# Moving shared experts, row sends and joins around the last sorting of a decoder layer

## The chip, the cores and the metric

The kernel runs on one core of a Trainium2 chip, as one program. The metric is the device time of one execution in microseconds, lower is better. The core has TensorE (PE), VectorE (DVE), ScalarE (ACT) and GpSimd (POOL), and SyncE (SP), which issues DMAs only. Each engine works through its own queue in order; the engines wait for each other by semaphores.

## The reference

One layer of a pre-norm decoder over 8 batches of 512 tokens of width 256, in float32. Three residual steps follow one another, each on the layer-normed x:

```
x = x + attn(layernorm(x))       # 16 heads: softmax over the tokens, causal convolution with it, output projection
x = x + xattn(layernorm(x), ctx) # causal cross attention over ctx_1024
x = x + ffn(layernorm(x))        # mixture of experts
```

The feed-forward part is where the change lies:

```
out    = sum over 2 shared experts of (silu(x wg_s) * (x wu_s)) wd_s          # width 128 each, for all tokens
probs  = softmax(x router_w)                                                  # 16 routed experts
weights, indices = top_k(probs, 2); weights = weights / (sum(weights) + 1e-9)
out   += sum over a token's 2 experts of weight * (silu(x wg_e) * (x wu_e)) wd_e   # width 64 each
```

## The kernel before, in words

**Batches.** A loop over the 8 batches runs the attention parts. The order inside an iteration is a written list of names (`ORDER`): steps of batch b (no sign), of the next one (`+`), and leftovers of the batch before (`-`). The leftovers are its shared experts (`-h0 -h1 -d0 -d1`), its ranking (`-rk`) and its sends (`-sd0` to `-sd7`).

**Shared experts** (`steps_shared`). Two steps `hidden` (gate and up matmuls, L614, a tanh, two scalings on VectorE, L618 and L619) and two steps `down` (L631), added into the batch's x tile. For batches 0 to 5 the x tile is then written out to DRAM (`kept`, L636).

**Routing.** A batch's tokens are ranked by expert (`ranked`, L554 to L580), and eight indirect DMAs on GpSimd (`send`, L588) put their normed rows into the DRAM buffer `xg` of their group, sorted by expert. Batches 0 to 5 are group 0, batches 6 and 7 group 1. When a group's last batch is ranked and sent, `tiled` and `tabled` (L645 to L706) work out a table of tiles of 128 rows, each of one expert: where its rows begin and which expert it has. This stretch, from the ranking to the first tile of a group, is called its sorting.

**Routed experts** (`steps_routed`). Tiles go four at a time (a quad): `fetch` loads the rows (`xs`, L718, on SP), `pick` copies the expert's gate and up weights (ScalarE, L727) and loads its down weights (`wdn`, L737, on SP and ScalarE), `turn` transposes the rows (L753), `hidden` and `down` are the matmuls (L772, L786), a scaling by the routing weight follows (L797, L799), and `put` (L807) writes the rows by indirect DMAs on GpSimd to `yg`, four for a quad, in the order of the tokens. Group 0 has 16 quads, group 1 has 8. The scaled rows of group 0 pass through 8 buffers (`y`).

**Joins** (`steps_join`). For a batch, `keep` loads the kept x again (L842), `take` loads its two rows for each token from `yg` (L851), `join` adds both on VectorE (L860) and writes the output (L861).

**Order around the change.** Where one list of steps is to be spread over another, `merged` interleaves them evenly and `idle(n)` puts in n empty places. The first six quads of group 0 run inside iteration 6, the next eight inside iteration 7 (the list `quads` counts pipeline steps: step q has the turn of q+1, the hidden of q, the down of q-1 and puts of q-1 and q-2). Behind the loop stands batch 7's sorting, with the rest of group 0, the shared experts of batches 6 and 7, and the first joins around it; then group 1's quads with the other joins; then group 1's own takes and joins. `tc.issue_after(x)` holds the steps under it behind instruction x. The written order sets priorities and dependences; a scheduler in the language orders each engine's queue from it when the program is built.

```
sorting = [last["rk"], *idle(3), *send, first1[0], *idle(0), *first1[1:-1], *idle(2), first1[-1]]
for f in merged(sorting, gap + sh, [*idle(0), *old[:5]]):
    f()
```

Here `first1` holds group 1's `tiled`, `tabled`, its first four fetches, `pick(0)` and `turn(0)`; `gap` is the rest of group 0's quads, `sh` the shared experts, `old` the keeps, takes and joins of group 0.

**Buffers that the change touches.** `xT` (4 buffers) holds transposed inputs, `h` (3) the hidden values of the shared experts and some temporaries, `wdn` (3) the down weights of a quad, and in PSUM `gu` (3) serves the hidden and down matmuls of shared and routed experts.

## Time and profile before

| what | us |
|---|---|
| median of 3 runs | 577.05 (573.98 to 578.42) |
| profiled execution | 575.53, of it the span 573.8 |
| PE busy | 508.6 (89% of the span) |
| DVE / POOL / ACT busy | 370.1 / 231.7 / 190.6 |
| mean granted PE clock | 0.949 of full speed |
| DMA | 107.67 MB, mean 188 GB/s |

The profile is one execution. In rows of a timeline the columns are start, length, engine, line, operation, tiles written and read, shape and count; the bracket holds the idle time of the engine just before and what ended it. In a table by stretches each row gives the length, then the busy time of PE, PE's weight loads, DVE, ACT and POOL, the granted PE clock, the share of time in which the DMA engines were busy, and GB/s. The slices of the page cut the span into 40 equal parts of 14.3 us, a digit for each in tenths. Issuing a DMA counts as busy on GpSimd only. Matmuls overlap at their ends, so their lengths add to more than their spacing.

### The profile page before, as it was taken

What the parts mean: (1) busy time and instruction counts of PE and PEld (TensorE: products, weight loads), DVE (VectorE), ACT (ScalarE), POOL (GpSimd) and SP (SyncE); (2) the same over time, 40 slices, a digit from 0 to 9 for tenths busy, and PEclk for the clock granted to TensorE, in tenths of its full rate; (3) what the DMA queues carried; (4) which work ended last, traced back from release to release, by engine and by line L of the source; (5) the groups of instructions that cost most, each with busy time, mean ns of one, the idle gap of its engine ahead of it and who ended that gap; (6) DMA issues with size and microseconds to landing.
All of it is one profiled execution on the core that took longest, in us unless ns stands there. A gap on an engine that the chain in (4) does not pass through costs nothing.

```text
span 573.8 us, 10065 instructions
## 1 busy us (share of the span) xinstructions
PE 508.6 (89%) x3172; PEld 337.0 (59%) x3172; DVE 370.1 (64%) x1290; ACT 190.6 (33%) x483; POOL 231.7 (40%) x257
## 2 busy tenths in 40 slices
PE   8989988999999999999999799999988986898720
PEld 5646626656666675774765367685766643486510
DVE  4348748868769778877876585546854682465343
ACT  2333303322333324224221335445455322156210
POOL 2300503432440640621433412454777577127780
PEclk8999999999999999999999799999999897899665
DMA  8880280751491392194182359756675143768966
GB/s 272 264 320 4 80 297 28 257 227 54 165 335 47 115 324 117 67 312 194 40 298 106 116 155 312 239 162 211 211 239 173 60 154 116 222 185 254 308 247 219
DMA packets 64108, 107.67 MB, mean 188 GB/s; under 512 B 8902, under 2 KB 37580, under 8 KB 63954
## 3 DMA queue, kind: packets, MB, share of 16 engines
q1 hardware_dynamic: 51672, 83.87, 44.4%
q0 software_dynamic: 7680, 16.87, 8.1%
q10 hardware_dynamic: 4704, 6.29, 3.3%
q8 instruction: 25, 0.41, 0.3%
q14 instruction: 27, 0.22, 0.1%
HBM read 82.35 MB, written 34.38 MB: 203 GB/s over the span
## 4 chain that ended last, share of the span: by engine, by line
PE 52%; DMA 17%; DVE 13%; POOL 7%; issue 5%; ACT 2%; SPq 2%; POOLq 0%; ACTq 0%; DVEq 0%
PE pc L398 6%; PE pd L631 4%; PE psc L450 4%; PE pa L479 4%; DMA T<-zd 4%; PE pgu L772 4%; PE pv L366 4%; PE pu L614 3%; PE pt L256 3%; PE pq L354 3%; POOL yg L807 3%; PE pv L338 3%; PE pg L614 3%; DMA xg<-row,place 3%; DMA yg<-y,to 3%
## 5 line engine op out<-in xcount | busy, mean ns | idle before, releaser
L807 POOL DMA_INDIRECT yg<-y,to x96 | 99.2, 1033 | 84.3 <-ACT y L797 50.3
L240 POOL TENSOR_TENSOR rs<-ve,power 128x2 f32<-128x2 f32 x48 | 35.4, 745 | 181.5 <-DVE ve L239 181.3
L588 POOL DMA_INDIRECT xg<-row,place x64 | 64.7, 1011 | 26.4 <-issue 16.2
L398 PE MATMUL pc<-T,vh 128*32 128x256 f32 (+1 forms) x512 | 58.1, 490 | 3.1 <-DMA T<-zd 1.6
L772 PE MATMUL pgu<-xsT,wgu 128*64 128x128 f32 x768 | 54.4, 284 | 2.6 <-DVE rh L776 2.1
L772 PEld LDWEIGHTS pgu<-xsT,wgu 128*64 128x64 f32 x768 | 44.7, 140 | 11.3 <-issue 7.8
L479 PE MATMUL pa<-v,pT 128*128 128x256 f32 x160 | 42.1, 394 | 0.0
L450 PE MATMUL psc<-kT,qT 128*128 128x128 f32 (+3 forms) x128 | 40.6, 441 | 0.7 <-DVE kT L261 0.7
L225 DVE BATCH_NORM_STATS2 bn<-x 128x6 f32<-128x256 f32 x96 | 37.7, 413 | 4.2 <-DMA x<-in_x_dram 3.2
L398 PEld LDWEIGHTS pc<-T,vh 128*32 128x32 f32 x512 | 19.0, 109 | 33.1 <-issue 19.0
L338 PE MATMUL pv<-wv_sb,xr 128*128 128x272 f32 (+1 forms) x128 | 34.1, 413 | 4.2 <-ACT xr L331 4.2
L786 PE MATMUL py<-wdn,rh 64*128 64x256 f32 x192 | 32.5, 428 | 5.7 <-DMA wdn<-wdn_d 4.9
L479 PEld LDWEIGHTS pa<-v,pT 128*128 128x128 f32 x160 | 30.1, 196 | 10.9 <-issue 3.8
L799 DVE TENSOR_SCALAR y<-py,w 128x256 f32<-128x256 f32 x48 | 22.2, 478 | 20.0 <-ACT y L797 12.7
L614 PE MATMUL pu<-x2T,wu_sb 128*128 128x512 f32 x64 | 32.0, 621 | 2.6 <-DVE h L618 2.6
L614 PE MATMUL pg<-x2T,wg_sb 128*128 128x512 f32 x64 | 32.7, 614 | 1.5 <-DVE h L618 1.5
L727 ACT COPY wgu<-wgu_r 128x256 f32 x96 | 32.2, 402 | 5.3 <-ACT rh L774 1.6
L631 PE MATMUL pd<-wd_sb,h 128*128 128x256 f32 x128 | 33.3, 387 | 0.5 <-DVE rh L776 0.5
L753 PE MATMUL pxt<-ident,xs 128*128 128x128 f32 x192 | 29.4, 288 | 4.3 <-DMA xs<-xg 3.8
L244 DVE TENSOR_SCALAR xn<-x,mv,rs 128x256 f32<-128x256 f32 x64 | 28.0, 475 | 6.4 <-POOL rs L240 5.5
L338 PEld LDWEIGHTS pv<-wv_sb,xr 128*128 128x128 f32 x128 | 24.8, 199 | 11.4 <-ACT xr L331 5.4
L432 PE MATMUL po<-wo_sb,oT 128*128 128x256 f32 x128 | 30.2, 389 | 1.0 <-DVE vh L343 1.0
(174 smaller groups left out, 913.5 us busy)
## 6 DMA issues: line engine op xcount, KB each, us to landing
T<-zd SPq DMA_DIRECT2D x32, 1024.0 KB
xs<-xg SPq DMA_DIRECT2D x96, 129.0 KB
x<-in_x_dram SPq DMA_DIRECT2D x8, 512.0 KB
ctxT<-in_ctxT_dram SPq DMA_DIRECT2D x8, 512.0 KB
yj_qT<-yg SPq DMA_DIRECT2D x8, 512.0 KB
yj_v<-yg SPq DMA_DIRECT2D x8, 512.0 KB
xg<-blank SPq DMA_DIRECT2D x6, 516.0 KB
kept<-x ACTq DMA_DIRECT2D x6, 512.0 KB
```

The costliest lines, as they stand in the source:

```text
L225: nc.vector.bn_stats(stats["bn"][:, c, :], src[:, c, :])
L240: st[b].setdefault(("pow", n), []).append(nc.gpsimd.tensor_tensor(stats["rs"][:, lo:hi], ve[:, lo:hi], power[:, lo:hi], ALU.pow).ins)
L338: nc.tensor.matmul(pv[:, :w], xr[:, k, i, :], wv_sb[:, k, :w], start=(k == 0), stop=(k == KC - 1))
L398: nc.tensor.matmul(s["pc"][o][32 * g:32 * g + 32, 2 * jp * P:], vh[:, jp, h, :], s["T"][h // HPT][:, h % HPT, :S - 2 * jp * P], start=(jp ...
L450: nc.tensor.matmul(pc[:, :w], s["qT"][:, k, i * P:w], s["kT"][:, k, :w], start=(k == 0), stop=(k == KC - 1))
L479: nc.tensor.matmul(pa[:, :D], s["pT", i][:, j * P:(j + 1) * P], s["v2"][:, j, :], start=(j == 0), stop=(j == i))
L588: ins = nc.gpsimd.indirect_dma_start(out=grp[g]["xg"][:, :], out_offset=bass.IndirectOffsetOnAxis(ap=s["place"][:, r, c:c + 1], axis=0), i ...
L614: nc.tensor.matmul(p, w[:, k, mt * P:(mt + 1) * P], s["x2T"][:, k, :], start=(k == 0), stop=(k == KC - 1))
L631: nc.tensor.matmul(pd[:, i, :], s["h", mt][:, c * P:(c + 1) * P], wd_sb[:, mt, :], start=(mt == 0), stop=(mt == NSH - 1))
L772: nc.tensor.matmul(p[o * MR:(o + 1) * MR, n, j, :], wgu[:, i, n, k, :], xT[:, k, i, :], start=(k == 0), stop=(k == KC - 1))
L786: nc.tensor.matmul(py[o][:, j, :], h[o * MR:(o + 1) * MR, j, :], wdn[o * MR:(o + 1) * MR, j, :], start=True, stop=True)
L807: ins = nc.gpsimd.indirect_dma_start(out=G["yg"][:, :], out_offset=bass.IndirectOffsetOnAxis(ap=G["to", q][:, i:i + 1], axis=0), in_=G["y" ...
```

## The change

Three lists and some tags change; no arithmetic does.

- The shared experts of batch 5 leave iteration 6 (before, they filled it as leftovers); those of batches 5, 6 and 7 run behind the loop: 5 beside batch 7's ranking and sends, 6 behind them, 7 among group 1's quads.
- Iteration 6 takes seven steps of group 0's quads in place of six, iteration 7 the next eight, so one less is left behind the loop.
- The x tile of batch 5 stays in its buffer (as those of 6 and 7 do), so it is neither kept out nor loaded again.
- Behind the loop the written order has the ranking, then at once the eight sends and group 1's table; `keep` and `take` of the first batches follow group 0's last puts; every join is held behind the last instruction of group 1's table.
- Every second `wdn` of group 1 uses an `h` buffer, and the kept tiles come back into two buffers (`xn1`, `ctxT`) in place of three.

```diff
+LATE = (5, 6, 7,)
+STAY = (5, 6, 7)
...
-                if cp == 1 and b in GROUPS[0]:
+                if cp == 1 and b not in STAY:
...
-        nc.vector.tensor_scalar_mul(G["col"], pt[:1, P:P + T], float(MR))
+        G["col_ins"] = nc.vector.tensor_scalar_mul(G["col"], pt[:1, P:P + T], float(MR)).ins
...
-                wdn = sb.tile([P, QT // 2, D], F32, tag="wdn", bufs=3, name=f"wdn{g}_{q}")
+                wdn = sb.tile([P, QT // 2, D], F32, tag="h" if g and q % 2 else "wdn", bufs=3, name=f"wdn{g}_{q}")
...
-                x = sb.tile([P, NT, D], F32, tag=("xn1", "ctxT", "oT")[bi % 3], bufs=1, name=f"xj{b}")
+                x = sb.tile([P, NT, D], F32, tag=("xn1", "ctxT")[bi % 2], bufs=1, name=f"xj{b}")
...
-                x, y = G["xj", bi] if g == 0 else st[b]["x"], G["yj", bi]
-                for r in range(2):
-                    nc.vector.tensor_tensor(x, x, y[r], ALU.add)
+                x, y = st[b]["x"] if b in STAY else G["xj", bi], G["yj", bi]
+
+                with tc.issue_after(grp[1]["col_ins"]):
+                    for r in range(2):
+                        nc.vector.tensor_tensor(x, x, y[r], ALU.add)
...
-        return [keep(bi) for bi in range(n) if g == 0], [take(bi) for bi in range(n)], [join(bi) for bi in range(n)]
+        return [keep(bi) for bi in range(n) if GROUPS[g][bi] not in STAY], [take(bi) for bi in range(n)], [join(bi) for bi in range(n)]
...
-        late = ("-h0", "-h1", "-d0", "-d1") if b == B - 1 else ()
+        late = ("-h0", "-h1", "-d0", "-d1") if b - 1 in LATE else ()
...
-            now = merged(now, first[:1] + idle(4) + first[1:-1] + idle(22) + first[-1:] + flat(quads[:6]))
+            now = merged(now, first[:1] + idle(4) + first[1:-1] + idle(26) + first[-1:] + flat(quads[:7]))
         elif b == 7:
-            now = merged(now, flat(quads[6:14]))
+            now = merged(now, flat(quads[7:15]))
...
-    gap = flat(quads[14:])
-    sh = [x[n] for x in (sh6, sh7) for n in ("h0", "h1", "d0", "d1")]
-    sorting = [last["rk"], *idle(3), *send, first1[0], *idle(0), *first1[1:-1], *idle(2), first1[-1]]
-    for f in merged(sorting, gap + sh, [*idle(0), *old[:5]]):
+    sh = [shared[b][n] for b in LATE for n in ("h0", "h1", "d0", "d1")]
...
+    old = []
+    for i in range(n):
+        if i + 2 < n:
+            old += [keeps[i + 2], takes[i + 2]]
+        old.append(joins[i])
...
+    rest = flat(quads[15:])
+    sorting = [last["rk"], *send, first1[0], first1[1], *idle(2)]
+    for f in merged(sorting, rest + sh[:4]):
+        f()
+    loads = [keeps[0], keeps[1], takes[0], takes[1], *idle(4), *old[:6]]
+    for f in merged([first1[2], *first1[-2:-1], *idle(2), first1[-1], *first1[3:-2]], sh[4:8], loads):
         f()
     keeps, takes, joins = steps_join(1)
-    for f in merged(flat(quads1), old[5:]):
+    for f in merged(flat(quads1), old[6:], sh[8:] + idle(3)):
         f()
-    for f in [*keeps, *takes, *joins]:
+    for f in [*takes, *joins]:
         f()
```

More of the change, by code (lines that the diff above doesn't have):

```diff
@@ L900, in flat @@
         return [f for y in x for f in y]
-    keeps, takes, joins = steps_join(0)
-    n = len(keeps)
-    old = [keeps[0], takes[0], keeps[1], takes[1]]
-    for i in range(n):
-        old.append(joins[i])
-        if i + 2 < n:
-            old += [keeps[i + 2], takes[i + 2]]
     for b in range(B):
@@ L922, in decoder_layer @@
             load_experts()
-    last, sh6, sh7 = backs[B - 1], shared[B - 2], shared[B - 1]
-    send = [last[f"sd{i}"] for i in range(8)]
-    gap = flat(quads[14:])
-    sh = [x[n] for x in (sh6, sh7) for n in ("h0", "h1", "d0", "d1")]
-    sorting = [last["rk"], *idle(3), *send, first1[0], *idle(0), *first1[1:-1], *idle(2), first1[-1]]
-    for f in merged(sorting, gap + sh, [*idle(0), *old[:5]]):
+    last = backs[B - 1]
+    sh = [shared[b][n] for b in LATE for n in ("h0", "h1", "d0", "d1")]
+    keeps, takes, joins = steps_join(0)
+    n = len(joins)
+    keeps += idle(n - len(keeps))
+    old = []
[3 more added lines that the diff above has]
+        old.append(joins[i])
+    send = [last[f"sd{i}"] for i in range(8)]
+    rest = flat(quads[15:])
[4 more added lines that the diff above has]
+    for f in merged([first1[2], *first1[-2:-1], *idle(2), first1[-1], *first1[3:-2]], sh[4:8], loads):
         f()
     keeps, takes, joins = steps_join(1)
-    for f in merged(flat(quads1), old[5:]):
+    for f in merged(flat(quads1), old[6:], sh[8:] + idle(3)):
         f()
-    for f in [*keeps, *takes, *joins]:
+    for f in [*takes, *joins]:
         f()
```

## The prediction

> **What bounds the kernel now.** I read the page first: busy shares, then the slices.
>
> ```profile
> PE 508.6 (89%) x3172; PEld 337.0 (59%) x3172; DVE 370.1 (64%) x1290; ACT 190.6 (33%) x483; POOL 231.7 (40%) x257
> ...
> PE   8989988999999999999999799999988986898720
> ...
> POOL 2300503432440640621433412454777577127780
> ```
>
> TensorE is the bound up to about slice 30; of its 65 us without work most lie behind that. So I went to the table by stretches (columns: PE, PEld, DVE, ACT, POOL busy, granted clock, DMA share, GB/s):
>
> ```profile
> 460.00:475.00 15.00, 11.68 (x70) 6.45 (x66) 11.62 (x57) 3.65 (x9) 10.50 (x10) 1.00 0.50 174
> 475.00:490.00 15.00, 9.97 (x29) 6.11 (x30) 4.83 (x15) 3.24 (x9) 10.47 (x11) 0.77 0.31 93
> ...
> 405.65:443.06 37.41, 34.51 (x300) 25.70 (x298) 23.47 (x82) 18.55 (x51) 29.29 (x30) 1.00 0.68 213
> 443.06:466.93 23.87, 20.55 (x178) 14.79 (x177) 16.40 (x68) 8.43 (x23) 13.67 (x16) 0.93 0.26 84
> ...
> 512.98:559.50 46.52, 29.05 (x276) 22.05 (x272) 24.32 (x47) 16.07 (x42) 35.50 (x32) 0.78 0.80 260
> ```
>
> The last row is group 1's 32 puts: 35.5 us of work plus 31 gaps of 0.30 are 44.8 of 46.5 us. From the first of them to the end **GpSimd's queue of puts is the bound**, then comes a tail. It was also full from 405 to 443 (29.3 + 29 x 0.30 = 38 of 37.4 us) and free again by 456. The timelines of GpSimd, VectorE and TensorE show what starts those 32 puts:
>
> ```profile
> 466.93 0.97 POOL L588 DMA_INDIRECT xg<-row,place  x1 [1.83 <-DVE row L579]
> ...
> 471.17 2.00 POOL L588 DMA_INDIRECT xg<-row,place  x1 [0.30 <-issue]
> ...
> 482.42 0.97 POOL L588 DMA_INDIRECT xg<-row,place  x1 [0.30 <-issue]
> ...
> 512.98 0.97 POOL L807 DMA_INDIRECT yg<-y,to  x1 [15.97 <-ACT y L797]
> ...
> 558.55 0.97 POOL L807 DMA_INDIRECT yg<-y,to  x1 [0.30 <-issue]
> ```
>
> ```profile
> 479.42 0.48 DVE L799 TENSOR_SCALAR y<-py,w 128x256 f32<-128x256 f32 x1 [5.86 <-DMA yg<-y,to]
> ```
>
> ```profile
> 480.03 0.37 PE L697 MATMUL ptab<-ident,row 128*1 128x128 f32 x1 [5.37 <-DVE row L685]
> ...
> 496.81 2.50 PE L614 MATMUL pu<-x2T,wu_sb 128*128 128x512 f32 x4 [2.63 <-DVE h L618]
> ...
> 499.95 1.70 PE L753 MATMUL pxt<-ident,xs 128*128 128x128 f32 x7
> ```
>
> In the last sorting a scaling of y stands in VectorE's queue until a put frees its buffer; the table behind it, and TensorE, lose 5.4 us. The rows of group 1 were fetched at 484.9, but TensorE turned them only at 499.95, behind two shared blocks and a join that held VectorE (2.6 us). After the last put the tail is 573.8 - 558.55 = 15.25 us.
>
> **The change, part by part.** Lengths are start to start in TensorE's timeline: a shared block has four groups of 1.72 (hidden) and 3.64 (down), 10.5 us; a quad of tiles has 1.02 turned, 1.9 hidden, 1.06 down, 4.0 us. The total work is the same; it is moved. Two DMAs of 0.5 MB go (kept out, kept in).
>
> *1. Iteration 6 loses shared block 5, and gets one more quad.* Of the 10.5 us, 5.2 (306.15 to 311.5) filled the first sorting, where the ranking's matmul waited 0.46 us for VectorE anyway. This cover goes: TensorE then waits some 3 us for the ranking, which comes perhaps 2 us earlier without two VectorE operations of 0.7 us; in the new order the first table also stands some eight convolutions earlier, and I give 1.5 us of this back. What is surely gained is the rest, 1.72 + 3.64 = 5.4 us. Against that the quad, 4.0. Sum: -0.5 - 5.4 + 4.0 = **-2 us** for batch 7's router transpose (456.2 to about 454).
> [...] after the 5.37 us wait the granted clock of 475:490 is 0.77, a pair of pg matmuls took 1.92 us in place of 0.96 and four pu 3.00 in place of 1.72, 2.2 us in all. [...] the row says up to 2.2. I take 0, and keep 2.2 for the range.
>
> *2. Sends.* The title has them follow the ranking, but in the built order all 64 puts of group 0 stand ahead of batch 7's eight sends on GpSimd (before: seven sends, then nine puts, one send among them). So 12 puts follow the down matmuls that stand before the router transpose: those begin near 453, and 12 x 1.285 gives 469 for the first send. Counted from the other end: from the first put (353.34) to the sends stand 72 puts and sends of 1.285 and 9.3 us of small operations, 102 us; before, GpSimd idled 21 us on this way, and with one more quad in a shorter iteration I expect 15: 470.5. I take 470; the ranks would be ready at 465 (466.9 - 2), so the queue binds. Seven steps of 1.285: the last send starts at 479.
> [...] By the row two sends beside batch 0's join took 1.39 and 2.00 in place of 0.97, 1.45 us in all, and the four joins among group 1's puts lengthened these by 1.07 each. I take 1.5, so **480.5 in place of 482.4**. The fetch came 2.5 us after the last send, and its data were used 4.1 us later (489.0): 487.
>
> *3. Joins behind the table, y before the ranking.* The stall of 5.86 us goes: y_15's scaling is issued before the ranking, and its buffers come free with the puts of tile 13, near 458. What is late next is not the table (ready near 472) but the sends. TensorE has shared blocks 5 and 6 there: from the rank matmul (461) 5.2 + 3.6 + 0.5 + 6.9 is 477, some 483 with the joins in VectorE's queue, which wait for 2 MB of takes (one take took 5.1 us). So the first turn starts with the data: **487 in place of 499.95**.
>
> *4. Shared block 7 among group 1's quads.* From the turn to the down matmuls of quad 0: 1.0 + 3.6 (down of block 6) + 1.0 + 1.9 + 3.4 (half of block 7) + 1.0 + 1.9 = 13.9, and 2.5 more to the first put, as before: 503.4 in place of 512.98, **-9.6**. Here comes the price. "gu" has three PSUM buffers. In the built placement pg and pu of block 7's second half hold two until its tanh, and that tanh writes an "h" buffer which the new wdn tiles share: it waits for quad 1's down. So hidden of quad 2 and both halves of quad 1's down pass through one buffer. By the rows (tanh 0.4, two scalings 0.9, y 0.45, join 1.2) TensorE loses some 4 us there; GpSimd waits 2.5 us before quad 1's puts, 3.6 before quad 2's (with 1.8 of down matmuls), 0.6 before quad 3's: 6.7. From quad 3 on a quad costs 4.0 on TensorE and 5.14 on GpSimd, so the puts bind again. 31 x 1.285 + 4 x 1.07 + 6.7 = 50.8, less some 1.7 where joins fall into waits: 49 in place of 45.6, **+3.5**. Last put at 552.4.
>
> *5. Edits with one answer.* One kept tile less saves 1 MB of some 20 MB behind 484, and no wait in the trace ends on it: 0. Buffers "xn1" and "ctxT" for joins: a load waits for the output before last; while puts bind: 0. First joins earlier: hidden. The tail waits for the last puts alone, 15.25 as before.
>
> **Sum:** 552.4 + 15.25 = 567.6, a span shorter by **6.2 us**. The profiled execution took 575.53 about its span of 573.8, the median of the runs is 577.05; from the median: **571 us**.
>
> **Rivals.**
> *A, more gain: block 7 hides beneath the puts.* GpSimd had 1.8 us of waiting in group 1 before, and if the single buffer costs no more, the last put comes at 503.4 + 45.6 = 549, some 3.4 us earlier: 567, or 564 if the queue at the sends is 2 us shorter. For it: TensorE has 29 us of work in 46.5. Against: a chain over three engines passes one buffer.
> *B, no change: iteration 6 gives nothing.* If the first ranking comes no earlier without its filler (-0.5 becomes +1.5) and the wait is paid with 2.2 us of half clock, the shift of -2 becomes +2, and everything behind follows: 575. For it: clock 0.67 to 0.70 and waits up to 1.5 us already stand at 320 to 334. That the sends don't follow the ranking belongs here: with the old 21 us of idle on GpSimd the first send comes at 475.6.
> *C, slower: SP's queue starves the turns.* Before, tiles 0 to 3 of group 1 were fetched with one take between them (484.9 to 505). Now a take, an output and a kept load stand between one fetch and the next, each waiting for a join or an earlier output while the fetches queue behind. To xs of quad 4 that is some 6.7 MB. At the 283 to 328 GB/s of 520 to 550 they take 24 us, and TensorE needs them 24 us after the first turn. It decides when they take 36 or more, under 190 GB/s: the last put then moves by 12 us and the end to 584. For it: a wdn load took 6.3 us at 521, with the DMA share above 0.9. Against: the rate.
>
> **How the numbers follow.** Forecast 571, its own range 566 to 576 (the send queue 2 us either way, the single buffer 3): 0.46. A 566: 0.20. B 575: 0.18. C 584: 0.16. A measurement of this kernel tells about 1%, 571.3 and 582.8. Faster: all of A and, the forecast lying at the bound, somewhat over half of its 0.46: 0.45. Same: the rest of the forecast and nearly all of B: 0.37. Slower: C and the end of B: 0.18. The range reaches from A's better end to the near side of C: 561 to 582.
>
> **What would show it.** Right: a wait of 2 to 4 us before the rank matmul near 308; batch 7's first send at 468 to 473, behind the last put and not behind a VectorE row; no 5 us wait at ptab; turn 0 at 484 to 490, released by xs; two waits for y before quads 1 and 2, then puts every 1.29 us; a tail of 15 us. Wrong: sends before 465 (A) or behind 474 (B), turns released by xs in quads 1 to 4 (C), or a tail of another length.

## The result, and the profile after

The changed kernel takes **582.53 us** (median of 9 runs, 579.05 to 586.14) against 574.18 us before (573.11 to 578.42): a ratio of **1.0128 (95% interval 1.0092 to 1.0163)**, slower by 1.3%, where 571 was forecast. The profiled execution has a span of 580.7 us (before 573.8, forecast 567.6).

The experiments fell on several chips. On two of them the kernel before takes some 615 us in place of 575, so every ratio below is to the kernel before on the same chip, and times are compared at one level only.

The page of the changed kernel: busy shares, then TensorE and GpSimd in 40 slices.

```profile
PE 507.4 (87%) x3172; PEld 334.8 (58%) x3172; DVE 372.5 (64%) x1290; ACT 189.5 (33%) x483; POOL 227.0 (39%) x257
...
PE   7889989999999999999996599999898896979820
...
POOL 3300404323431540640634203565677573024770
```

TensorE's work is what it was. GpSimd's slices 34 to 37 read 3 0 2 4 where before they read 7 1 2 7: it idles longer around the start of group 1's puts. The table by stretches of the changed kernel (columns: PE, PEld, DVE, ACT, POOL busy, clock, DMA share, GB/s):

```profile
460.00:475.00 15.00, 14.01 (x54) 7.42 (x50) 11.85 (x63) 3.62 (x8) 11.34 (x13) 0.89 0.07 20
...
510.91:566.58 55.67, 36.98 (x312) 26.64 (x310) 25.03 (x53) 16.96 (x45) 32.95 (x32) 0.85 0.66 209
```

The stall in the last sorting is gone: 460 to 475 has 14.0 us of TensorE work (before 11.7). But the 32 puts of group 1 now lie in 55.7 us (before 46.5), with less GpSimd work in them (33.0 for 35.5) and 8 us more of TensorE. GpSimd's timeline has the ends:

```profile
474.95 0.96 POOL L592 DMA_INDIRECT xg<-row,place  x1 [0.31 <-issue]
...
483.78 1.03 POOL L592 DMA_INDIRECT xg<-row,place  x1 [0.30 <-issue]
510.91 0.98 POOL L811 DMA_INDIRECT yg<-y,to  x1 [26.11 <-ACT y L801]
...
522.21 0.97 POOL L811 DMA_INDIRECT yg<-y,to  x1 [6.47 <-ACT y L801]
...
533.62 0.97 POOL L811 DMA_INDIRECT yg<-y,to  x1 [5.86 <-ACT y L801]
...
565.62 0.97 POOL L811 DMA_INDIRECT yg<-y,to  x1 [0.30 <-issue]
```

Against before, the first put comes 2.1 us earlier (510.91 for 512.98), from first to last put it takes 9.1 us longer (54.71 for 45.57), and the tail is 15.1 us for 15.25: +6.9 us, which is the whole difference of the spans. Two long waits, before the puts of quads 1 and 2 (522.21 and 533.62), take 12.3 us; the kernel before has one wait of 1.8 us in this stretch. TensorE's timeline shows what they wait for:

```profile
490.20 0.33 PE L757 MATMUL pxt<-ident,xs 128*128 128x128 f32 x1 [1.30 <-DMA xs<-xg]
...
493.07 4.90 PE L635 MATMUL pd<-wd_sb,h 128*128 128x256 f32 x16
498.40 1.13 PE L757 MATMUL pxt<-ident,xs 128*128 128x128 f32 x6 [0.43 <-DMA xs<-xg]
...
514.61 0.66 PE L757 MATMUL pxt<-ident,xs 128*128 128x128 f32 x4 [1.47 <-DMA xs<-xg]
515.10 1.88 PE L618 MATMUL pu<-x2T,wu_sb 128*128 128x512 f32 x4
516.92 1.97 PE L776 MATMUL pgu<-xsT,wgu 128*64 128x128 f32 x32
520.32 1.10 PE L790 MATMUL py<-wdn,rh 64*128 64x256 f32 x4 [1.44 <-issue]
...
522.51 1.66 PE L790 MATMUL py<-wdn,rh 64*128 64x256 f32 x4 [0.28 <-DVE y L803]
...
526.16 3.68 PE L776 MATMUL pgu<-xsT,wgu 128*64 128x128 f32 x32 [1.38 <-DVE h L622]
```

A row released by xs is a turn whose rows are not there: those of quad 0 at 490, of quad 1 at 498 and of quad 3 at 514. Behind the waits of 490 to 492 and of 526 TensorE runs slower: 3.68 us at 526.16 for a pgu group that takes 1.97 at 516.92 (granted clock 0.50 for 1.00), 4.90 at 493.07 for 16 pd of which eight take 1.99 at 529.77 (0.74 for 1.00). Behind the wait of 1.47 us at 514.61 it does not: four pu in 1.88. The mean clock of the last stretch is 0.85. Block 7's pu stands between the late turn of quad 3 and the hidden of quad 2 (516.92).

The chain that the prediction gave is there as well. The down matmuls of quad 1 go in two halves (520.32 and 522.51), the second behind VectorE's reading of the first. Only behind them comes the second tanh of block 7, which writes an `h` buffer that quad 1's down weights had; ScalarE's row shows it:

```profile
524.21 0.60 ACT L621 ACTIVATE h<-pg 128x512 f32<-128x512 f32 x1 [2.27 <-PE py L790]
```

And the hidden matmuls of quad 3 (526.16) wait 1.38 us for the scaling L622 behind this tanh. They do not read its result; it reads block 7's `pg` and so stands between them and a `gu` buffer.

SP's queue, which issues those rows, in the changed kernel:

```profile
488.05 1.91 SPq L722 DMA_DIRECT2D xs<-xg  x4
490.75 1.15 SPq L741 DMA_DIRECT2D wdn<-wdn_d  x2
492.00 0.59 SPq L855 DMA_DIRECT2D yj_qT<-yg  x1
492.69 0.40 SPq L855 DMA_DIRECT2D yj_v<-yg  x1
493.63 4.25 SPq L722 DMA_DIRECT2D xs<-xg  x4
497.93 0.43 SPq L867 DMA_DIRECT2D out_dram<-xj  x1
498.89 1.05 SPq L722 DMA_DIRECT2D xs<-xg  x2
501.25 0.33 SPq L846 DMA_DIRECT2D xj<-kept  x1
501.77 0.85 SPq L722 DMA_DIRECT2D xs<-xg  x2
...
505.14 6.36 SPq L722 DMA_DIRECT2D xs<-xg  x4
```

and in the kernel before:

```profile
491.14 7.94 SPq L718 DMA_DIRECT2D xs<-xg  x12
```

Before, quads 1 to 3 are issued in one go, from 6.2 to 14.2 us after quad 0's start at 484.91. After, two takes (the second at 502.72), an output, a kept load and two weight loads stand between them, and the last of quad 3's goes out by 511.50, 23.4 us after quad 0's start.

### The profile page after: what moved, and what is told of

Read it like the earlier page. It is cut to its first block, busy times and chain, and to the rows that moved or that the text cites. A ratio compares the mean times of both kernels' runs of the same rounds, so it can differ in the third digit from the quotient of the medians.

```text
span 580.7 us, 10046 instructions
## 1 busy us (share of the span) xinstructions
PE 507.4 (87%) x3172; PEld 334.8 (58%) x3172; DVE 372.5 (64%) x1290; ACT 189.5 (33%) x483; POOL 227.0 (39%) x257
## 5 line engine op out<-in xcount | busy, mean ns | idle before, releaser
L811 POOL DMA_INDIRECT yg<-y,to x96 | 96.1, 1001 | 95.2 <-ACT y L801 70.4
L592 POOL DMA_INDIRECT xg<-row,place x64 | 63.2, 988 | 24.9 <-issue 16.6
L402 PE MATMUL pc<-T,vh 128*32 128x256 f32 (+1 forms) x512 | 60.4, 512 | 3.2 <-DMA T<-zd 2.5
L776 PE MATMUL pgu<-xsT,wgu 128*64 128x128 f32 x768 | 53.4, 283 | 4.0 <-DVE rh L780 1.6
L757 PE MATMUL pxt<-ident,xs 128*128 128x128 f32 x192 | 30.8, 286 | 6.5 <-DMA xs<-xg 4.9
L790 PE MATMUL py<-wdn,rh 64*128 64x256 f32 x192 | 31.2, 405 | 4.0 <-issue 1.4
L757 PEld LDWEIGHTS pxt<-ident,xs 128*128 128x128 f32 x192 | 21.9, 143 | 19.7 <-issue 8.2
L618 PE MATMUL pu<-x2T,wu_sb 128*128 128x512 f32 x64 | 30.5, 596 | 3.0 <-DVE x L637 1.8
L358 PE MATMUL pq<-ctxT,qk_sb 128*128 128x512 f32 x64 | 30.4, 594 | 0.0
## 6 DMA issues: line engine op xcount, KB each, us to landing
T<-zd SPq DMA_DIRECT2D x32, 1024.0 KB, 10.9
```

Source lines behind the costliest of these rows:

```text
L402: nc.tensor.matmul(s["pc"][o][32 * g:32 * g + 32, 2 * jp * P:], vh[:, jp, h, :], s["T"][h // HPT][:, h % HPT, :S - 2 * jp * P], start=(jp ...
L592: ins = nc.gpsimd.indirect_dma_start(out=grp[g]["xg"][:, :], out_offset=bass.IndirectOffsetOnAxis(ap=s["place"][:, r, c:c + 1], axis=0), i ...
L618: nc.tensor.matmul(p, w[:, k, mt * P:(mt + 1) * P], s["x2T"][:, k, :], start=(k == 0), stop=(k == KC - 1))
L757: nc.tensor.transpose(pt[:, i * P:(i + 1) * P], xs[:, i, 2 + k * P:2 + (k + 1) * P], ident)
L776: nc.tensor.matmul(p[o * MR:(o + 1) * MR, n, j, :], wgu[:, i, n, k, :], xT[:, k, i, :], start=(k == 0), stop=(k == KC - 1))
L790: nc.tensor.matmul(py[o][:, j, :], h[o * MR:(o + 1) * MR, j, :], wdn[o * MR:(o + 1) * MR, j, :], start=True, stop=True)
```

## The experiments

All milestones in one table, from the profiles at the level of 575 us, in order of their telling ("first turn" is TensorE's first transpose of group 1's rows):

| kernel | first turn | first put | last put | first to last | tail | ratio to before (95%) |
|---|---|---|---|---|---|---|
| before | 499.9 | 513.0 | 558.5 | 45.6 | 15.2 | 1 |
| changed | 490.2 | 510.9 | 565.6 | 54.7 | 15.1 | 1.0128 (1.0092 to 1.0163) |
| c_after2 (changed again) | 489.8 | 510.7 | 563.4 | 52.7 | 15.4 | 1.0082 (1.0047 to 1.0117) |
| g1_block5_back | 485.6 | 511.9 | 564.4 | 52.4 | 16.7 | 1.0116 (1.0053 to 1.0179) |
| g2_block7_last | 489.4 | 506.6 | 561.5 | 54.9 | 15.4 | 1.0067 (1.0034 to 1.0100) |
| g3_best | 488.2 | 509.5 | 559.7 | 50.2 | 15.2 | 0.9912 (0.9880 to 0.9944) |
| h1_fetches_first | 496.6 | 509.6 | 559.2 | 49.6 | 15.2 | 1.0057 (1.0032 to 1.0083) |
| h2_fetches_first_last7 | 497.5 | 507.7 | 561.7 | 54.0 | 15.1 | 1.0048 (1.0026 to 1.0070) |
| h5_all_three | 486.5 | 505.4 | 558.8 | 53.4 | 21.5 | 1.0146 (1.0115 to 1.0177) |
| h3_best_sends_first | 482.5 | 508.4 | 559.4 | 51.1 | 16.4 | 0.9993 (0.9974 to 1.0011) |
| f5_y15_joins | 487.7 | 512.3 | 558.7 | 46.4 | 15.1 | 0.9986 (0.9966 to 1.0005) |
| f2b_block7_among | 488.6 | 507.8 | 559.7 | 51.9 | 15.1 | 1.0040 (1.0011 to 1.0068) |

### First suspects: shared buffers, one PSUM buffer, the clock, block 7's place

The theory at that point was the prediction's own: block 7 passes through too few buffers. Four edits of the changed kernel, on a chip where the kernel before takes 615 us.

**e1_wdn_own.**

```diff
-tag="h" if g and q % 2 else "wdn", bufs=3
+tag="wdn", bufs=3
```

> The changed kernel with one edit: all down weights of group 1 in the three wdn buffers again, none in h. Theory 1 (the stalls among group 1's quads come from block 7's second half, whose tanh waits for quad 1's down because they share an h buffer, so that two of the three gu banks stay taken): the waits of 6.5 and 5.9 us before the puts of quads 1 and 2 shrink to 2 to 4 us each, and the end comes 3 to 6 us earlier than the changed kernel (577 to 580 against 582.5). Rival (the rows xs arrive late behind takes and outputs on SP's queue): no change beyond 1 us. Rival (three gu banks are too few for eleven more tenants, whoever waits): under 2 us.

**e2_mm_banks.**

```diff
-pg = ps.tile([P, 512], F32, tag="gu", bufs=3, name=f"pg{b}_{mt}")
+pg = ps.tile([P, 512], F32, tag="mm" if b == 7 else "gu", bufs=3, name=f"pg{b}_{mt}")
...
```

> The changed kernel with block 7's gate, up and down results in the three PSUM banks mm, which nothing uses among group 1's quads, in place of gu; the shared h buffer stays. Theory 1: the quads keep gu for themselves, the waits before the puts of quads 1 and 2 fall to under 3 us each, and the end comes 5 to 8 us earlier (575 to 578). Rival (xs late): the waits stay with xs as their releaser, under 2 us of gain. If both e1 and e2 gain, the chain h buffer to bank is the cause; if only e2 does, the banks alone.

**e3_fill_first** (its five extra matmuls are not part of the computation).

```diff
             nc.tensor.transpose(pl[:, :P], s["lT"], ident)
+            if b == 5:
+                fill = ps.tile([P, 512], F32, tag="gu", bufs=3, name="fill")
+                for _ in range(5):
+                    nc.tensor.matmul(fill, ones, s["x2T"][:, 0, :], start=True, stop=True)
```

> The changed kernel with five matmuls 128x512 more, of no use, behind batch 5's router transpose, where TensorE waits 4.75 us for the ranking; they write a gu bank that nothing reads. Theory 2 (the wait that opened when block 5 left the first sorting slows the clock, and the convolutions behind it ran at half rate: 5.35 us for 32 passes): the convolution after it takes about 2.8 us again, the conv-bound wait of 4.2 us before pv shrinks, batch 7's router transpose comes 2 to 4 us earlier (455 to 456.5) and the end 2 to 3 us earlier (579.5 to 580.5). Rival (the wait itself costs, the clock nothing): no change.

**e4_block7_in_sorting.**

```diff
-... first1[-1], *first1[3:-2]], sh[4:8], loads):
+... first1[-1], *first1[3:-2]], sh[4:], loads):
...
-merged(flat(quads1), old[6:], sh[8:] + idle(3))
+merged(flat(quads1), old[6:])
```

> The changed kernel with shared block 7 back in the last sorting, behind block 6, so that nothing of the shared experts is left among group 1's quads. Theory 1 (block 7 among the quads costs 9 us from first to last put): from first to last put 45 to 47 us again in place of 54.7; the first put comes later by the block's first half less what the wait for xs hides, 5 to 8 us (516 to 519), the end at 577 to 581. Rival (the stretch from first to last put is long for other reasons: xs behind takes): it stays above 51 and the end comes later than the changed kernel, 585 or more.

**c_after** is the changed kernel itself, run later on another chip of the same level.

> The changed kernel itself, as the control for the runs beside it. Every theory expects a ratio to the kernel before of 1.013 (1.009 to 1.016 measured before), the last put some 7 us later, from a first put about 2 us earlier and 9 us more from the first put of group 1 to the last. If the ratio is below 1.005 here, the loss depends on the chip or the run and the comparisons must be made within one chip only.

Measured: c_after 1.0025 (0.9991 to 1.0059), e1 1.0021 (0.9993 to 1.0049), e2 1.0059 (1.0029 to 1.0088), e3 1.0045 (1.0012 to 1.0078); e4 617.44 us over 4 runs, against 615.39 before, too few for a ratio. No edit beats the control. The chain of the prediction is in c_after, and e1 takes it out: the second tanh of block 7 waits for quad 1's down matmuls in c_after and comes right behind its own matmuls in e1. ScalarE's row in c_after, then in e1:

```profile
554.47 0.60 ACT L621 ACTIVATE h<-pg 128x512 f32<-128x512 f32 x1 [1.74 <-PE py L790]
```

```profile
541.44 0.60 ACT L621 ACTIVATE h<-pg 128x512 f32<-128x512 f32 x1 [0.91 <-issue]
```

The waits before the puts of quads 1 and 2 fall with it from 9.0 us to 6.9, but the later ones grow from 6.9 to 11.0: the puts take 57.0 us from first to last (control 55.8, e2 58.1). So on these chips taking the chain out gains nothing. Since the whole change costs 0.25% there, with an interval that reaches below 1, this does not settle the level of 575 us, where neither edit was run alone. In e4 block 7 stands in the sorting again; the first put comes at 546.8 (control 543.6) and first to last is 51.8, so the last put is 0.7 us earlier (598.6 for 599.3). TensorE's timeline of e3:

```profile
313.34 0.43 PE L570 MATMUL pk<-both,before 128*128 128x64 f32 x2 [1.32 <-DVE both L568]
...
313.93 4.08 PE L402 MATMUL pc<-T,vh 128*32 128x512 f32 x48
...
328.37 1.12 PE L260 MATMUL pt<-ident,xn 128*128 128x128 f32 x4 [4.33 <-ACT xnT L263]
```

Behind the filler the convolutions run faster: 48 matmuls in 4.08 us, 85 ns each, where the changed kernel has 32 in 5.35, 167 ns each, at a granted clock of 0.50 (mean of 300 to 340 us: 0.87 in e3, 0.83 in c_after and in the changed kernel). It buys nothing: the convolutions are through 4 us earlier than in c_after (322.2 for 326.2), but then TensorE waits 4.33 us for ScalarE, and group 0's first put comes at 356.0 (c_after 356.7).

### Parts of the change, alone on the kernel before (615 us)

**f1_block5_late** (step 1):

```diff
-                if cp == 1 and b in GROUPS[0]:
+                if cp == 1 and b < 5:
...
-        late = ("-h0", "-h1", "-d0", "-d1") if b == B - 1 else ()
+        late = ("-h0", "-h1", "-d0", "-d1") if b >= B - 2 else ()
...
-... idle(22) + first[-1:] + flat(quads[:6]))
+... idle(26) + first[-1:] + flat(quads[:7]))
...
-    gap = flat(quads[14:])
-    sh = [x[n] for x in (sh6, sh7) for n in ("h0", "h1", "d0", "d1")]
+    gap = flat(quads[15:])
+    sh = [x[n] for x in (shared[5], sh6, sh7) for n in ("h0", "h1", "d0", "d1")]
```

> The kernel before with step 1 alone: shared block 5 goes from iteration 6 into the last sorting, one quad more in iteration 6, the x tile of batch 5 stays. Theory (iteration 6 gives nothing): rank matmul of batch 5 at the same time as before with a wait of 4 to 5 us in front of it, router transpose of batch 7 later by 1 to 3 us, and the last sorting has 10.5 us of shared block more and 4.0 us of quad less, of which the 5.4 us wait can take some: first turn of group 1 later by 3 to 8 us, time 1.005 to 1.014 of before. Rival (my prediction's step 1): transpose of batch 7 2 us earlier, first turn later by 0 to 4, ratio 1.000 to 1.007.

**f2_block7_among** (step 4):

```diff
-    sh = [x[n] for x in (sh6, sh7) for n in ("h0", "h1", "d0", "d1")]
+    sh, among = [[x[n] for n in ("h0", "h1", "d0", "d1")] for x in (sh6, sh7)]
...
-    for f in merged(sorting, gap + sh, [*idle(0), *old[:5]]):
+    for f in merged(sorting, gap + sh + idle(4), [*idle(0), *old[:5]]):
...
-    for f in merged(flat(quads1), old[5:]):
+    for f in merged(flat(quads1), old[5:], among + idle(3)):
```

> The kernel before with step 4 alone: shared block 7 goes from the last sorting to group 1's quads. Theory (block 7 costs GpSimd's queue as much as it frees): first turn of group 1 some 10 us earlier (490), first put 5 to 9 us earlier, two waits of about 6 us before quads 1 and 2 and first to last put 53 to 55 in place of 45.6, so the last put within 2 us of before: ratio 0.996 to 1.004. Rival P (the prediction's step 4): first to last 49 and ratio 0.988 to 0.993. Rival D (the long waits come only from the edits beside it: block 6, joins and late fetches there): first to last 46 to 48, ratio 0.985 to 0.990.

**f3_joins_behind** (the hold of step 3):

```diff
+                with tc.issue_after(grp[1]["col_ins"]):
                     for r in range(2):
                         nc.vector.tensor_tensor(x, x, y[r], ALU.add)
```

> The kernel before with the hold of step 3 alone: joins of group 0 behind the last instruction of group 1's table; the scaling of y_15 still waits for a put. Theory: the lengthened sends (1.39 and 2.00 for 0.97) become normal, the last send 1.5 us earlier, the wait of 5.9 us for y stays (it is the buffer's, not the join's), the 2.6 us wait that a join causes before pu may go or move: first turn 0 to 3 us earlier, ratio 0.996 to 1.000. Rival 1 (the hold is what removes the 5.9 us stall): turn 4 to 6 us earlier, 0.990. Rival 2 (the joins pile up among group 1's puts and lengthen them): ratio 1.002 to 1.006.

Measured: f1 **1.0107** (1.0078 to 1.0135), f2 0.9998 (0.9963 to 1.0033), f3 0.9938 (0.9909 to 0.9967). f1 lands in the theory's band: step 1 alone costs. TensorE's timeline of f1 has the wait that block 5 had covered:

```profile
311.93 0.69 PE L562 MATMUL pk<-both,before 128*128 128x64 f32 x2 [4.75 <-DVE both L560]
```

f2 gains nothing, against the prediction's own -6 us. f3 lies between the band of its theory (0.996 to 1.000) and rival 1 (0.990). With block 7 in the sorting, the puts take 51.0 us from first to last in f1 and 54.2 in f3, so at this level they are long without it too. The three parts add up to +0.43% where the whole has 0.25% on this chip: within the intervals.

### Undoing parts, at the level of 575 us

**c_after2** is the changed kernel once more.

> The changed kernel once more, as the control for the runs beside it. If the kernel before takes some 575 us here, the ratio is 1.013 as first measured; if it takes some 615 us, 1.0025 as in the earlier control (0.9991 to 1.0059).

**g1_block5_back** (step 1 undone):

```diff
-LATE = (5, 6, 7,)
+LATE = (6, 7,)
-STAY = (5, 6, 7)
+STAY = (6, 7)
...
-... idle(26) + first[-1:] + flat(quads[:7]))
+... idle(22) + first[-1:] + flat(quads[:6]))
...
-    sh = [shared[b][n] for b in LATE for n in ("h0", "h1", "d0", "d1")]
+    sh = idle(4) + [shared[b][n] for b in LATE for n in ("h0", "h1", "d0", "d1")]
-    rest = flat(quads[15:])
+    rest = flat(quads[14:])
```

> The changed kernel with step 1 alone undone: block 5 back in iteration 6, six and eight quads in the loop, x of batch 5 kept out again. Theory (step 1 is the loss, the rest is worth a little): router transpose of batch 7 2 to 3 us earlier than in the control, first turn of group 1 earlier by 4 to 8 us, ratio to before 0.990 to 0.997, that is 0.8 to 1.5% under the control. Rival (step 4 is the loss, step 1 costs at most 2 us): within 0.4% of the control.

**g2_block7_last**:

```diff
-tag="h" if g and q % 2 else "wdn", bufs=3
+tag="wdn", bufs=3
-                    y = sb.tile([P, QT, D], F32, tag="xT", bufs=4, name=f"y{g}_{q}")
+                    y = sb.tile([P, QT, D], F32, tag="xs", bufs=3, name=f"y{g}_{q}")
...
-    for f in merged(flat(quads1), old[6:], sh[8:] + idle(3)):
+    for f in merged(flat(quads1), old[6:], idle(4) + sh[8:] + idle(2)):
```

> The changed kernel with block 7 later: its four steps stand between the hidden of quad 3 and the down of quad 6 in place of quads 0 to 4 (wdn in its own buffers, y of group 1 in the free xs buffers, which the move needs). Theory T (TensorE, not a buffer, starves GpSimd: 10.5 us of block 7 fall on the first quads, where TensorE has a slack of only 1.1 us a quad over the puts): the two waits of 4 to 6 us before the puts of quads 1 and 2 go, the first put comes 2 to 4 us earlier since half a block stood before it, first to last put 46 to 50 in place of 55, ratio 0.99 of the control or less (5 to 9 us). Rival (single buffers, late fetches or the joins make the waits): they stay where they are, within 0.4% of the control.

**g3_best**, on the kernel before: the hold of f3, the move of f2 with `idle(4) + among + idle(2)`, y of group 1 in "xs" as in g2, and

```diff
-                if g == 0:
+                if g == 0 and q < 15:
                     y = [sb.tile([P, D], F32, tag="y", bufs=8, ...
```

> The kernel before with what the runs so far speak for: joins behind the table, y of group 0's last quad in a buffer of its own kind (so that its scaling does not hold VectorE for 5.9 us), block 7 late among group 1's quads; block 5 stays in iteration 6. Theory: no 5 us wait at ptab, first turn some 10 us earlier, first to last put within 3 us of the kernel before, ratio 0.975 to 0.985. Rival (the puts of group 1 wait for TensorE wherever block 7 stands): ratio 0.992 to 0.998, as f3_joins_behind.

Measured: g1 1.0116, no better than its control's 1.0082; that is what the rival said. Its milestones follow the theory as far as the first turn: batch 7's router transpose at 455.0 (control 458.6), the first turn at 485.6 (489.8). Then TensorE stands, in g1:

```profile
485.56 2.28 PE L757 MATMUL pxt<-ident,xs 128*128 128x128 f32 x8 [10.33 <-DMA xs<-xg]
...
501.48 0.69 PE L757 MATMUL pxt<-ident,xs 128*128 128x128 f32 x2 [4.58 <-DMA xs<-xg]
```

and SP's queue in g1 says why: three takes stand ahead of quad 1's rows, which go out 12.6 us after quad 0's.

```profile
483.38 1.90 SPq L722 DMA_DIRECT2D xs<-xg  x4
488.14 0.33 SPq L855 DMA_DIRECT2D yj_qT<-yg  x1
...
493.82 0.32 SPq L855 DMA_DIRECT2D yj_qT<-yg  x1
494.87 0.32 SPq L855 DMA_DIRECT2D yj_v<-yg  x1
496.01 5.09 SPq L722 DMA_DIRECT2D xs<-xg  x4
```

So the first put comes at 511.9, later than in the control. In g2 the first put comes 4.1 us earlier, as theory T said, but most of the waits only move: 4.9, 3.9 and 3.1 us before quads 1, 3 and 4, first to last 54.9. Late rows and late down weights have a part in them, so this does not show block 7 as the one cause. In time (1.0067) it is 0.15% under the control, as its rival said. g3 is at 0.9912, faster than both kernels, by less than the theory gave.

### Fetches first

Still open was whether SP's queue or block 7 holds the puts, and whether the two hide each other. All three kernels below carry this edit of the changed kernel:

```diff
-    loads = [keeps[0], keeps[1], takes[0], takes[1], *idle(4), *old[:6]]
-    for f in merged([first1[2], *first1[-2:-1], *idle(2), first1[-1], *first1[3:-2]], sh[4:8], loads):
+    loads = [keeps[0], keeps[1], takes[0], takes[1]]
+    for f in merged([first1[2], *first1[3:-2], *first1[-2:]], sh[4:8], loads):
...
-    for f in merged(flat(quads1), old[6:], sh[8:] + idle(3)):
+    for f in merged(flat(quads1), old, sh[8:] + idle(3)):
```

> The changed kernel with one list reordered: the first four fetches of group 1 stand at once behind each other, and only the first two takes before them; the other kept loads, takes, joins and outputs come behind, among the quads. Theory S (SP's queue: in the changed kernel takes, an output and a kept load stand between these fetches, so TensorE gets quads 1 and 2 late and down of quad 0, which stands behind their turns, waits with them): from the first turn to the first put 16 to 18 us in place of 20.8, first put 3 to 5 us earlier, end 3 to 5 us earlier: on a chip where the kernel before takes 575 us a ratio of 1.000 to 1.005 (control 1.008 to 1.013), on one of 615 us 0.995 to 0.999 (control 1.0025). Rival B7 (block 7's 10.5 us on TensorE decide): the first put moves, but the last put by less than 1 us: ratio as the control.

**h2_fetches_first_last7** adds g2's three lines.

> The same with block 7 late among the quads as well (as in g2_block7_last, which alone gave 0.15% over its control). Theory S+B7 (each one hides the other: with late rows the early block costs nothing, with early rows the late block can hide): first put 13 to 15 us after the first turn (as in the kernel before), first to last put 46 to 50, end 8 to 12 us before the control: ratio 0.988 to 0.998 at 575 us. Rival: no more than the sum of h1_fetches_first and g2_block7_last.

**h5_all_three** adds g1's lines to h2.

> The same, and step 1 undone as well (block 5 back in iteration 6; alone this moved the first turn 4.6 us earlier, but not the end, since rows came late). Theory (step 1 costs 4 to 5 us of the first turn once nothing behind it waits for rows): end 4 to 5 us before h2_fetches_first_last7, ratio 0.980 to 0.990 at 575 us. Rival (the puts are bound from further back, step 1 costs nothing): within 0.3% of h2_fetches_first_last7.

**h3_best_sends_first** is g3_best with

```diff
-sorting = [last["rk"], *idle(3), *send, first1[0], *idle(0), *first1[1:-1], *idle(2), first1[-1]]
+sorting = [last["rk"], *send, *idle(6), first1[0], *first1[1:-1], *idle(1), first1[-1]]
```

> g3_best (0.991) with the table's steps written later, so that the last send no longer stands behind four puts of group 0 on GpSimd. Theory: last send at 477 to 479 in place of 483.6, first turn of group 1 at 482 to 484 in place of 488.2, ratio 0.980 to 0.987 at 575 us. Rival (the rows of quads 1 to 3 and the puts behind set the end, not the first turn, as undoing step 1 showed): ratio within 0.3% of 0.991.

Measured: h1 1.0057 (1.0032 to 1.0083). Its rows go out in one go, and no turn of group 1 waits for rows; SP's queue and TensorE's in h1:

```profile
487.20 9.45 SPq L722 DMA_DIRECT2D xs<-xg  x16
```

```profile
496.63 1.04 PE L757 MATMUL pxt<-ident,xs 128*128 128x128 f32 x8
```

The first turn comes later than in the control, because block 6's down matmuls now stand ahead of it, so turn to put (13.0 us for 20.8) can't be compared; the first put is 1.1 us earlier, where theory S had 3 to 5. The waits before quads 1 and 2 fall from 10.9 to 7.0 us, and the last put comes at 559.2 in place of 563.4 (565.6 in the first profile). The tanh of block 7 still waits for quad 1's down (1.74 us) in h1: the chain is in what is left. The time follows by 0.25% against c_after2 and 0.7% against the first measurement; against the former the intervals overlap. Theory S stands in the trace, and accounts for a part of the loss only. h2 adds nothing (1.0048, where its theory had 0.998 at most): the two together gain no more than their parts. h5 has the earliest first put of all (505.4) and a last put as early as before, but the held joins, now all written behind the fetches, come out last. VectorE's last row in h5:

```profile
574.98 1.23 DVE L866 TENSOR_TENSOR x<-x,yj_v 128x1024 f32<-128x1024 f32 x1 [3.03 <-DMA yj_v<-yg]
```

The tail is 21.5 us, with joins of group 0 and group 1 in it, and the ratio 1.0146. h3 has the last send at 477.8 (g3 483.6) and the first turn at 482.5, 17 us before that of the kernel before; its last put comes at 559.4, and it is level with it (0.9993). Both outcomes go against the theories written for them.

### Which edit of g3 counts

**f5_y15_joins** is the hold of f3 with `q < 15` as in g3. **f2b_block7_among** is f2 again.

> The kernel before with joins behind the table and y of group 0's last quad in a buffer of its own kind, that is g3_best without block 7's move (block 7 stays in the last sorting). Theory (moving block 7 among group 1's quads gains nothing on the whole: what the first turn wins, the puts wait for again): within 0.3% of g3_best, on a chip of 575 us 0.988 to 0.994; first turn later than in g3_best by 5 to 9 us (493 to 497), first to last put 45 to 47 in place of 50.2. Rival (block 7's move made g3_best's gain): 0.997 to 1.001.

> Step 4 alone on the kernel before once more (0.9998 on a chip where it takes 615 us). Theory, as for the other run: first turn some 8 to 10 us earlier, waits of 7 to 12 us in group 1's puts, ratio 0.997 to 1.003. Rival P (the prediction's step 4: 6.7 us of waits and 9.6 us gained): 0.988 to 0.993. Rival W (the move costs more than it frees, and is what makes the changed kernel slower): 1.006 to 1.012.

Measured: f5 0.9986 (0.9966 to 1.0005), f2b **1.0040** (1.0011 to 1.0068). f5 misses its theory's 0.988 to 0.994 and lies in the band of its rival, that block 7's move made g3's gain. f5 removes the stall of 5.9 us and the join's, and has its first transpose 12 us earlier, but the other seven only from 499.96 on, behind blocks 6 and 7; TensorE's and GpSimd's rows in f5:

```profile
487.68 0.48 PE L753 MATMUL pxt<-ident,xs 128*128 128x128 f32 x1 [9.55 <-DMA xs<-xg]
```

```profile
512.27 0.97 POOL L807 DMA_INDIRECT yg<-y,to  x1 [14.09 <-ACT y L797]
```

The 5.4 and 2.6 us that TensorE lost before became one wait of 9.55 us for the first rows, because the rest of block 6 and all of block 7 stand behind this transpose in TensorE's queue. The first put is where it was (512.3 for 513.0). In f2b the first turn is 11.4 us earlier, the first put 5.2, and the last put 1.2 us later; GpSimd's rows:

```profile
507.82 0.97 POOL L807 DMA_INDIRECT yg<-y,to  x1 [9.83 <-ACT y L797]
...
543.94 0.97 POOL L807 DMA_INDIRECT yg<-y,to  x1 [6.04 <-ACT y L797]
```

So step 4, done alone, does not gain its -6 us; it costs 0.4%, a little over its theory's band (0.997 to 1.003), which the interval reaches. The wait of 6.04 us is a chain over three queues, of which VectorE's and TensorE's rows in f2b show two:

```profile
531.81 1.23 DVE L860 TENSOR_TENSOR xj<-xj,yj_qT 128x1024 f32<-128x1024 f32 x1 [2.97 <-DMA xs<-xg]
```

```profile
534.98 0.66 PE L772 MATMUL pgu<-xsT,wgu 128*64 128x128 f32 x2 [4.43 <-DVE rh L776]
```

VectorE stands for 2.97 us ahead of the first add of a join. The profile names the rows xs as what came last, but this add reads a kept tile and a take, so it is more likely the take, issued at 524.95, that was late. Then both adds go through between the scalings of the hidden values, and TensorE waits 4.43 us for these and goes on more slowly (two transposes in 0.69 us at 535.57, in 0.44 at 497.36). The kernel before has a wait of 1.82 us at this place (542.3), f5 one of 4.33.

## Why the prediction was wrong

The forecast span was 567.6, the measured one 580.7. The 13.1 us split by the prediction's own steps: first turn +3.2 (490.2 for 487), turn to first put +4.3 (20.7 for 16.4), first to last put +5.7 (54.7 for 49), tail -0.1.

*Step 1* failed in sign. Batch 7's router transpose came at 458.5, not 454; four other profiles with this loop have 457.8 to 459.5, two with step 1 undone 455.0 and 455.8, five with the loop of before 456.2 to 458.0. The term that failed is "comes perhaps 2 us earlier": the rank matmul came at 311.76 (before 312.14), so the wait was 4.75 us and not 3. And behind it came a slower clock, for which I had taken 0 (my estimate, which no trace showed): the granted clock from 312.81 to 318.16 was 0.50. TensorE's rows in the changed kernel:

```profile
311.76 0.69 PE L566 MATMUL pk<-both,before 128*128 128x64 f32 x2 [4.75 <-DVE both L564]
...
312.81 5.35 PE L402 MATMUL pc<-T,vh 128*32 128x512 f32 x32
```

The same matmuls take 2.78 us for 30 some 7 us later (granted clock 1.00), so 32 would be 2.97: a price of 2.4 us, near the 2.2 that the row of before gave and I kept for the range alone. Behind a wait of the same length the 32 took 4.08 us in f1, 4.26 in c_after2 and 4.81 in h1, so the wait alone does not fix the price. But e3, where they take 85 ns each, gains nothing, so the clock alone is not what failed. The other wrong term is "what is surely gained". The table by stretches has 300 us to group 0's first put, before and changed:

```profile
300.00:353.34 53.34, 47.50 (x297) 30.04 (x296) 35.00 (x142) 19.00 (x51) 13.70 (x14) 0.94 0.51 158
```

```profile
300.00:354.79 54.79, 42.74 (x280) 27.40 (x279) 32.66 (x137) 17.61 (x49) 13.70 (x15) 0.88 0.46 146
```

TensorE has 4.8 us less work there and yet takes 1.5 us longer: it stands for 12.1 us where it stood for 5.8, so its work did not set the length of this stretch, and taking block 5 out of it could not shorten it. The prediction's terms give -2.2 for it. From there to the router transpose one quad stands for block 5's down matmuls: +0.9, where the terms give +0.4. At the end of the kernel, though, step 1 cannot be told at 575 us: with it undone, the time it won was lost to rows that came late (g1) or to the tail (h5). On the kernel before, at 615 us, it costs 1.1%.

*Step 2* was right in mechanism: the sends follow the last of the 12 puts with gaps of 0.30, and nothing waits for ranks. The first came at 474.95, not 470, which is step 1's 4.5 us handed on (g1, with step 1 undone, has 469.4), and near the 475.6 of rival B. The two joins beside the sends were priced at 1.5 us; beside those at 480.00 and 482.75 (1.25 and 1.23 us long) each send took 0.96 to 1.03, as the others did (0.96). So the last send was only 3.3 us later than forecast.

*Step 3*: the stall went, as said; the table had no wait. What was late next was named (the sends), but f5 shows that the gain was not there to be had alone.

*Step 4* is the step that failed most. Two terms were mis-sized. The 13.9 us from the first turn to the first down took 18.8: the turn of quad 0 took 2.9 in place of 1.0, as its rows came tile by tile, block 6's down matmuls 5.3 in place of 3.6, the turns of quads 1 and 2 1.8 and 1.5 in place of 1.0. And the waits of 2.5, 3.6 and 0.6 before the puts of quads 1 to 3 were 6.5 and 1.0, 5.9, and 1.1: 14.4 in place of 6.7; the 4 x 1.07 of joins came to 1.8. The chain that I gave as the reason stands in the trace (524.21, 526.16). What I had put at nothing is that the rows come late: with the rows in time, in h1, the same waits are 4.1 and 0.5, 2.9, and none, 7.5 us, near my 6.7. Of the 14.4, some 5 to 7 us thus go with the late rows and the slower matmuls behind them (12.5 in c_after2). That is an estimate, since h1 also moves block 6 ahead of the first turn.

In f2b, with nothing else changed, the same terms read: first turn 488.6 (487), turn to first put 19.2 (16.4), waits of 2.4, 0.5, 1.2 and 0.9 before quads 1 to 4, less than the 6.7, and then the 6.0 before quad 5, which I had not seen; first to last +6.3 (+3.5). So block 7's own waits were sized fairly there too; the forecast missed late rows, late takes and late scalings, and slower matmuls behind some waits: behind that of 4.43 us two transposes took 0.69, behind one of 3.08 at 495.60 they took 0.42. I had written that TensorE had 29 us of work in 46.5. But a quad costs TensorE 4.0 us and GpSimd 5.14, so over seven quads the slack is 8 us, and 8 us more of TensorE stand among the changed kernel's puts: nothing is left for anything late. That this is why each delay comes through is argued, not shown. The ten profiles at 575 us with block 7 among the quads, early or late, take 49.6 to 54.9 us from first to last put; the two without it 45.6 and 46.4.

*Step 5*: right; tail 15.1.

Rival C had the cause and not the place. SP's queue starves the turns, but those of quads 1 and 3, not of quad 4, for 4 to 6 us at the last put (h1) and not 12. What I set against it, the rate of the transfers, did not bear on it: the order in which SP issues them did. Two of my signs of being wrong came: the first send behind 474 (B) and turns released by xs in quads 1 and 3 (C).

**What stays open.** Against a loss of 0.8 to 1.3%, step 4 alone on the kernel before costs 0.4%, and the order of the fetches in the changed kernel 0.25 to 0.7%; step 1 alone costs 1.1% at 615 us and was not run alone at 575. These parts need not add up, and the rest was not isolated. What the chain through the `h` and `gu` buffers costs at 575 us is open. The gain of g3 is measured but not explained: its profiled run was the slowest of its seven (576.65 us; the median is 570.71) and shows no milestone that f5 or h3 lacks, and h3, its near relative, did not repeat it. f5 points to a version that was not tried: blocks 6 and 7 ahead of the first turn, in the 9.55 us in which TensorE waits there.

## What to carry to other kernels

Before a block of work is taken out to save time, look whether its engine sets the length of that stretch: here 4.8 us less of TensorE's work made it no shorter. Before a block is moved under another engine's queue, its length is to be set against the slack of the pair (here 1.14 us a quad), not against the idle share of a stretch; here the puts took 49.6 to 54.9 us from first to last with the block among them, early or late, and 45.6 and 46.4 without it (all at 575 us). A stall that is taken out of an in-order queue gains only if what stands behind it is ready (in f5, 5.4 and 2.6 us of waiting became one wait of 9.55): look which wait ends next, and whether work that could fill it stands behind the waiting instruction. When loads move, read the order on the issuing queue first: in g1 three takes ahead of a fetch put it 12.6 us behind the one before it.

## What the runs showed of the hardware

The same kernel, the one before, takes 574.7 to 575.2 us (medians) on three chips and 615.4 and 615.8 on two others. Up to 355 us the profiles nearly agree (group 0's first put at 354.8 in the changed kernel, 356.7 in c_after); of the 34 us by which c_after's profile is longer, 25 come among the routed quads of group 0: batch 7's router transpose is at 485.8 in place of 458.5. The mean granted clock is 0.927 there and 0.953 in the first profile. The chain of waits of TensorE from 355 to 460 in c_after (us in total, times, longest) begins with

```profile
PE pgu L776 <- issue: 13.2, 14, 1.8
```

a wait that the profile puts down to no engine and no DMA; in the changed kernel's first profile no such line stands there. What it is was not tested. The effect of an edit differs between the two levels: the whole change is 1.0025 there and 1.008 to 1.013 at 575 us, and the hold of the joins, 0.9938 there, came to 0.9986 here with a second edit beside it.
